# Four stacked graph layers on one core: a plan that counts changes of TensorE's tiling, and pairs a graph's scores with an older graph's weights times v

## The chip, the core and the metric

The kernel runs on one core of a Trainium2 chip. The metric is the device time of one execution in microseconds. A core has TensorE (matrix products into PSUM), VectorE (called DVE in the profile), ScalarE (ACT), GpSimd (POOL), and SyncE (SP), which here issues most DMAs. The engines run side by side, each through its own list of instructions in a fixed order, and wait for each other through semaphores.

## What is computed

There are 128 graphs of 128 nodes with 512 features, float32, and one adjacency matrix for all. Four layers follow each other; each ends in a residual sum and a normalisation over the features.

```
x = layernorm(x + L0(x))   # A = adj @ x; per node: relu(max over features of A + b)
x = layernorm(x + L1(x))   # h = x @ W; e = leaky_relu(s1 + s2) * adj; att = softmax(e)
                           # elu(att @ h + beta * h)
x = layernorm(x + L2(x))   # (adj @ x) @ weight + bias
x = layernorm(x + L3(x))   # q, k, v = x @ Wq + bq, ...; 8 heads of 64
                           # scores = q @ k.T / 8, masked where adj == 0
                           # softmax(scores) @ v
```

## The kernel before

Graphs pass through the layers one after the other in a pipeline. For a graph b, TensorE runs these steps: `l0` (one product of 128x512), `zT` (four products of 128x128 that apply the attention of layer 1 and transpose), `z` (four products of 128x512 with W), `yT` and `y` (the same pair for layer 2), then for each group of four graphs 21 steps named q, k and v, which make the three projections by seven half-size products each (`seven`), and for each graph the scores, `sc`, and the product of the softmax weights with v, `avT`. An instruction of the program is run by TensorE as two in the profile[...].

Two of these steps use half of TensorE's array at a time. In `l3_scores` (line 785) a head has 64 features, so a product uses 64 of the 128 rows, and two heads lie in the two halves of the rows. In `l3_avT` (line 871) the result of a head has 64 columns, and two heads lie in the two halves of the columns. Every other step uses the whole array. The last six graphs (`LATE`) take another way behind the scores: `l3_pT` (line 849) transposes their weights on TensorE, and `l3_av` (line 917) multiplies them in whole-array products of 65 columns.

Between `sc` and `avT` of one graph lies a long way. VectorE adds the mask to the scores (line 807, which frees the single PSUM tile of the scores and fills the single buffer `pr`) and takes each row's maximum (line 813). ScalarE takes eight exponentials (line 817). SyncE writes the weights to HBM and reads them back in another order (lines 366 and 370). VectorE finishes the transposition (line 377) into one of two buffers `pT`. After `avT`, ScalarE copies the result (line 883), it goes through HBM and VectorE in the same manner, GpSimd scales it and adds the residual (lines 896 and 897), and the last normalisation follows.

The order on every engine comes from a planner, the class `Plan`, that runs while the program is built. It keeps a clock for TensorE and simulates the other engines with a cost for each of their operations. Every step has a place in line, an expected cost, the marks (results) that it waits for, and the buffers that it takes. In `Plan.run` the clock picks, of all steps that are ready by the plan's own times, the one with the smallest place; then it adds the cost. The other engines' operations are emitted in the order in which they begin in the plan. A step's place is its graph's number plus its turn, then its position in a row:

```
row = ["av", "sc", "yT", "y", "l0", "zT", "z"]
turns = {"av": 12.5, "sc": 11.5, "yT": 3, "y": 3, "l0": 0, "zT": 2, "z": 2}
return lambda b: (b + turns[name]) * R + row.index(name)
```

So weights times v of a graph are due one round after its scores, where a round is what TensorE does for one graph. They run when the plan has them ready.

Of the kernel before, what the change touches and what calls it, by code (L numbers as in the profile page):

```python
# [22 lines left out]
class Plan:  # L23

    def __init__(self, bufs):
        self.heap, self.count = [], 0  # L30
        self.engine = {}
        self.left = dict(bufs)
        self.parked = {tag: [] for tag in bufs}
        self.marks, self.waiting = {}, {}
        self.end = 0.0
# [56 lines left out]
    def run(self, steps, total):  # L92

        nxt = {name: 0 for name in steps}
        now = 0.0
        while any(nxt[name] < total[name] for name in steps):
            self.events(now)
            best, later = None, []
            for name, (place, cost, waits, bufs, fn) in steps.items():
                b = nxt[name]  # L100
                if b >= total[name]:
                    continue
                marks = [self.marks.get(key) for key in waits(b)]
                if any(m is None for m in marks) or any(self.left[t] < n for t, n in bufs(b).items()):
                    continue
                if marks and max(marks) > now:
                    later.append(max(marks))
                elif best is None or place(b) < best[0]:
                    best = (place(b), name, b)
            if best is None:  # L110
                if self.heap:
                    later.append(self.heap[0][0])
                now = min(later)
                continue
            _, name, b = best
            place, cost, waits, bufs, fn = steps[name]
            nxt[name] += 1
            for tag, n in bufs(b).items():
                self.left[tag] -= n
            now += cost  # L120
            self.end = now + HOP
            gen = fn(b)
            self.resume(gen, self.end)
        self.events(float("inf"))
# [3 lines left out]
def kernel(  # L128
# [815 lines left out]


    row = ["av", "sc", "yT", "y", "l0", "zT", "z"]
    turns = {"av": 12.5, "sc": 11.5, "yT": 3, "y": 3, "l0": 0, "zT": 2, "z": 2}
    R = len(row)

    def place(name):  # L950
        return lambda b: (b + turns[name]) * R + row.index(name)
# [4 lines left out]
    def av_waits(b):  # L956
# [12 lines left out]
        "xT": (early("y", 1.0), 0.55, lambda b: [("x3", b)], need("mm"), l3_xT),  # L969
        **{n: (seven_place(n), 1.73, seven_waits(n), seven_bufs(n), seven(n)) for n in "qkv"},  # L970
        "sc": (
            place("sc"), 1.1,
            lambda b: [(n, b // GB, "C", r, b % GB // 2) for n in "qk" for r in range(2)],
            need("sc"), l3_scores,
        ),
# [48 lines left out]
```

## Time and profile before

| | |
|---|---|
| median of three runs | 2804.46 us (2802.49 to 2806.31) |
| profiled execution | 2803.4 us |
| its span, first to last instruction | 2801.6 us |
| mean granted clock of TensorE | 0.992 |
| TensorE busy | 2730.6 us, 97% |
| VectorE busy | 2276.3 us, 81% |
| ScalarE busy | 1573.6 us, 56% |
| GpSimd busy | 1388.1 us, 50% |
| mean busy share of the DMA engines | 47% between 100 and 2700 us |

A busy share is the time in which an engine had an instruction running, over the span. The ends of matmuls are modelled, and consecutive ones overlap[...]; the starts of matmuls are what was measured. A wait is put down to the engine and the instruction that ended it. The profile's rows name a tile by its name in the program without its number: `ps_sc` are the scores, `ps_av` weights times v, `ps_q_chain` and its like the projections, `psA` layer 0.

### The profile page before, as it was taken

What the parts mean: (1) busy time and instruction counts of PE and PEld (TensorE: products, weight loads), DVE (VectorE), ACT (ScalarE), POOL (GpSimd) and SP (SyncE); (2) the same over time, 40 slices, a digit from 0 to 9 for tenths busy, and PEclk for the clock granted to TensorE, in tenths of its full rate; (3) what the DMA queues carried; (4) which work ended last, traced back from release to release, by engine and by line L of the source; (5) the groups of instructions that cost most, each with busy time, mean ns of one, the idle gap of its engine ahead of it and who ended that gap; (6) DMA issues with size and microseconds to landing.
All of it is one profiled execution on the core that took longest, in us unless ns stands there. A gap on an engine that the chain in (4) does not pass through costs nothing.

```text
span 2801.6 us, 42968 instructions
## 1 busy us (share of the span) xinstructions
PE 2730.6 (97%) x13905; PEld 1936.2 (69%) x13905; DVE 2276.3 (81%) x4288; ACT 1573.6 (56%) x4189; POOL 1388.1 (50%) x2192
## 2 busy tenths in 40 slices
PE   6999999999999999999999999999999999999997
PEld 3677677777667666776776776776777677676776
DVE  7668888888888878888888888988888888888866
ACT  3455555555555555555555555555655555555545
POOL 4535444555445545445545455554554554455545
PEclk8999999999999999999999999999999999999998
DMA  3224444455444445445444445454454444444443
GB/s 123 59 84 140 147 130 140 142 156 152 141 149 139 144 129 158 147 138 153 149 143 152 141 144 160 144 160 145 142 162 139 134 137 148 143 147 142 138 132 125
DMA packets 459793, 392.26 MB, mean 140 GB/s; under 512 B 88752, under 2 KB 376624, under 8 KB 459568
## 3 DMA queue, kind: packets, MB, share of 16 engines
q1 hardware_dynamic: 456464, 383.74, 44.8%
q10 hardware_dynamic: 2976, 5.77, 0.6%
q8 instruction: 110, 1.80, 0.3%
q14 instruction: 115, 0.94, 0.1%
q0 software_dynamic: 128, 0.01, 0.0%
HBM read 218.17 MB, written 171.24 MB: 139 GB/s over the span
## 4 chain that ended last, share of the span: by engine, by line
PE 85%; DVE 11%; POOL 1%; DMA 1%; issue 1%; ACT 1%; SPq 0%; DVEq 0%; POOLq 0%; ACTq 0%
PE ps_z L508 14%; PE ps_y L508 13%; PE ps_q_chain L681 7%; PE ps_k_chain L681 7%; PE ps_v_chain L681 7%; PE ps_av L871 4%; PE ps_sc L785 4%; PE ps_zT L494 4%; PE ps_k_pair L681 4%; PE ps_v_pair L681 4%; PE ps_q_pair L681 3%; PE psA L390 3%; PE ps_yT L551 3%; PE ps_q_first L681 2%; DVE pT L377 2%; PE ps_v_first L681 2%
## 5 line engine op out<-in xcount | busy, mean ns | idle before, releaser
L350 POOL TENSOR_SCALAR ve<-mv 128x1 f32<-128x1 f32 x512 | 129.7, 253 | 821.8 <-DVE mv L347 723.7
L508 PE MATMUL ps_y<-w_sb,yT 128*128 128x512 f32 x1024 | 463.8, 596 | 0.5 <-ACT yT L557 0.5
L508 PE MATMUL ps_z<-w_sb,zT 128*128 128x512 f32 x1024 | 462.6, 594 | 1.6 <-ACT zT L500 1.1
L817 ACT ACTIVATE pr<-pr,nm 128x128 f32<-128x128 f32 x992 | 387.1, 393 | 77.8 <-DVE nm L813 76.8
L356 ACT ACTIVATE x<-xp,nmr,rstd 128x512 f32<-128x512 f32 x384 | 311.0, 810 | 187.8 <-POOL nmr L354 184.4
L345 DVE BATCH_NORM_STATS2 stats<-xp 128x6 f32<-128x512 f32 x512 | 345.0, 674 | 23.2 <-ACT xp L399 14.7
L508 PEld LDWEIGHTS ps_z<-w_sb,zT 128*128 128x128 f32 x1024 | 192.4, 190 | 211.0 <-issue 203.2
L508 PEld LDWEIGHTS ps_y<-w_sb,yT 128*128 128x128 f32 x1024 | 190.7, 190 | 201.6 <-issue 193.2
L352 POOL TENSOR_TENSOR rstd<-ve,nhalf 128x1 f32<-128x1 f32 x512 | 298.6, 583 | 42.7
L377 DVE STREAM_TRANSPOSE pT<-turn_pr 128x1024 f32<-128x1024 f32 x122 | 249.7, 2047 | 0.0
L412 DVE SCALAR_TENSOR_TENSOR junk<-x,wa_bc 128x512 f32<-128x512 f32 x256 | 208.5, 814 | 50.7 <-ACT x L356 49.0
L896 POOL TENSOR_TENSOR xp<-xp,rd 128x512 f32<-128x512 f32 x122 | 128.2, 1050 | 233.0 <-DVE xp L377 153.1
L521 ACT ACTIVATE elu_r<-ps_z 128x512 f32<-128x512 f32 x128 | 76.1, 594 | 269.8 <-PE ps_z L508 269.5
L537 POOL TENSOR_TENSOR x2b<-x,bias_bc 128x512 f32<-128x512 f32 x128 | 164.4, 1284 | 113.8 <-ACT x L356 109.9
L639 POOL TENSOR_TENSOR x3r<-x3r,bv_bc 128x512 f32<-128x512 f32 x128 | 170.5, 1332 | 90.3 <-DMA x3r<-turn_hbm_x 89.2
L817 ACT ACTIVATION_READ_ACCUMULATOR pr<-pr,nm 128x1 f32 x976 | 185.1, 190 | 0.0
L354 POOL TENSOR_SCALAR nmr<-mv,rstd 128x1 f32<-128x1 f32 x512 | 147.4, 288 | 53.0
L525 DVE SCALAR_TENSOR_TENSOR xp<-ps_z,x 128x512 f32<-128x512 f32 x128 | 87.8, 686 | 95.2 <-ACT elu_r L521 95.1
L897 POOL TENSOR_TENSOR xp<-xp,x3r 128x512 f32<-128x512 f32 x122 | 159.6, 1308 | 9.6
L785 PEld LDWEIGHTS ps_sc<-kTh,qTh 64*128 64x128 f32 x2048 | 124.2, 187 | 52.3 <-issue 32.2
L871 PE MATMUL ps_av<-pT,va 128*64 128x128 f32 x1952 | 135.4, 281 | 21.6 <-DVE pT L377 17.1
L871 PEld LDWEIGHTS ps_av<-pT,va 128*64 128x64 f32 x1952 | 105.9, 138 | 72.9 <-issue 30.6
(148 smaller groups left out, 5929.6 us busy)
## 6 DMA issues: line engine op xcount, KB each, us to landing
turn_hbm_pr<-pr SPq DMA_DIRECT2D x122, 512.0 KB
turn_pr<-turn_hbm_pr SPq DMA_DIRECT2D x122, 512.0 KB
x<-in_x_dram SPq DMA_DIRECT2D x128, 256.0 KB
out_dram<-xp SPq DMA_DIRECT2D x128, 256.0 KB
turn_hbm_x<-x SPq DMA_DIRECT2D x124, 256.0 KB
turn_x<-turn_hbm_x SPq DMA_DIRECT2D x124, 256.0 KB
x3r<-turn_hbm_x SPq DMA_DIRECT2D x124, 256.0 KB
turn_hbm_o<-oT SPq DMA_DIRECT2D x122, 256.0 KB
```

The lines of the kernel that those rows point to most:

```text
L345: nc.vector.bn_stats(stats, src)
L352: nc.gpsimd.tensor_tensor(rstd, ve, nhalf, ALU.pow)
L356: nc.scalar.activation(dst, src, AF.Identity, bias=nmr, scale=rstd)
L377: nc.vector.transpose(dst.rearrange("p n (c a) -> p a n c", a=NQ), t)
L412: nc.vector.scalar_tensor_tensor(junk, x1, 1.0, wa_bc[i], ALU.mult, ALU.mult, accum_out=col)
L508: nc.tensor.matmul(ps, lhsT(c), rhs(c), start=(c == 0), stop=(c == NCC - 1))
L537: nc.gpsimd.tensor_tensor(xb, x2, bias2_bc, ALU.add)
L639: nc.gpsimd.tensor_tensor(s["x3r"], s["x3r"], by_block(b, bv_bc), ALU.add)
L681: nc.tensor.matmul(ps[:, m, :], lhsT, rhs, start=fresh and m + k == 0, stop=m + k == 2, skip_group_check=not fresh)
L785: nc.tensor.matmul(ps[:, h % 2, f, :], heads["q", g][j // 2][r : r + HD, f, j % 2 * P : (j % 2 + 1) * P], heads["k", g][j // 2][r : r + HD ...
L817: nc.scalar.activation(pr_h[:, i], pr_h[:, i], AF.Exp, bias=nm[:, i : i + 1], accum_out=None if late else den[:, i : i + 1])
L871: nc.tensor.matmul(ps[e * HD : (e + 1) * HD, f * P : (f + 1) * P], va[:, 2 * f + e, 0:HD], pT[:, e * 4 + f, :], start=True, stop=True,)
```

## The change

Two of the planner's steps are declared half-array ones, `sc` of rows and `avT` of columns. The planner remembers which use of the array the last step left (`mode`), and adds 0.2 us to its clock whenever the next step has another. After a half-array step it prefers a half-array step if one is ready, one of the same kind first, and only then goes by place; after a whole-array step it goes by place as before. The turn of `av` goes from 12.5 to 14.5, so that weights times v are due three rounds after the scores, and the planned cost of `sc` from 1.1 to 0.92. No operation of any engine is edited.

```diff
+    TILED = {"sc": "rows", "avT": "columns"}
+    SWITCH = 0.2
...
-        now = 0.0
+        now, mode = 0.0, None
...
-                elif best is None or place(b) < best[0]:
-                    best = (place(b), name, b)
+                else:
+                    tiled = self.TILED.get(name)
+                    key = ((tiled is None, tiled != mode) if mode else (), place(b))
+                    if best is None or key < best[0]:
+                        best = (key, name, b)
...
-            now += cost
+            now += cost + (self.SWITCH if self.TILED.get(name) != mode else 0.0)
+            mode = self.TILED.get(name)
...
-    turns = {"av": 12.5, "sc": 11.5, "yT": 3, "y": 3, "l0": 0, "zT": 2, "z": 2}
+    turns = {"av": 14.5, "sc": 11.5, "yT": 3, "y": 3, "l0": 0, "zT": 2, "z": 2}
...
-            place("sc"), 1.1,
+            place("sc"), 0.92,
```

The diff adds nine lines ahead of the steps, so line 871 of before is line 880 after, and so on.

## The prediction

> **What bounds the kernel now.** I read the page first (engines, slices), then TensorE's waits, then its timeline around single blocks, then VectorE's timeline there.
>
> ```profile
> span 2801.6 us, 42968 instructions
> PE 2730.6 (97%) x13905; PEld 1936.2 (69%) x13905; DVE 2276.3 (81%) x4288; ACT 1573.6 (56%) x4189; POOL 1388.1 (50%) x2192
> PE   6999999999999999999999999999999999999997
> ```
>
> TensorE is busy in every slice but the first and last; the next engine, VectorE, has a fifth of its time free. So a microsecond of TensorE's own queue is a microsecond of the end, as long as what it reads arrives. "Busy" says nothing of how well it is used, so I looked at start times. In this stretch of TensorE's timeline (start, length, line, tiles):
>
> ```profile
> 1418.85 1.89 PE L681 MATMUL ps_v_chain<-sums_v,T 128*128 128x256 f32 x8
> 1420.58 1.02 PE L390 MATMUL psA<-x,adjT 128*128 128x512 f32 x2
> 1421.53 1.16 PE L785 MATMUL ps_sc<-kTh,qTh 64*128 64x128 f32 x16
> 1422.62 1.16 PE L494 MATMUL ps_zT<-attT,x 128*128 128x128 f32 x8
> 1423.71 1.09 PE L871 MATMUL ps_av<-pT,va 128*64 128x128 f32 x16
> 1424.73 1.16 PE L551 MATMUL ps_yT<-adjT,x 128*128 128x128 f32 x8
> 1425.73 1.89 PE L681 MATMUL ps_v_pair<-wv_sb,xTh 128*128 128x256 f32 x8
> 1427.46 1.02 PE L508 MATMUL ps_z<-w_sb,zT 128*128 128x512 f32 x2
> ```
>
> The lengths are modelled; the distances of starts are what the queue pays. Nothing waits here. A layer-0 product (psA) between whole-array steps takes 0.858 start to start; ahead of the scores it takes 0.95, so 0.094 more. A transposing step of eight (zT, yT) between whole-array steps takes 0.891; yT, right behind a half-array step, takes 1.00, so 0.104 more; zT, with one on both sides, takes 1.09, both surcharges. A seven-product step shows the same over the trace: 1.727 alone, 1.820 ahead of, 1.831 behind a half-array step. The scores take 1.09 and weights times v 1.02 wherever they stand. **A visit to half use therefore costs 0.198 us outside its own steps.**
>
> What a second half-array step costs when it follows directly is shown elsewhere in the same view:
>
> ```profile
> 1484.05 1.16 PE L785 MATMUL ps_sc<-kTh,qTh 64*128 64x128 f32 x16
> 1485.14 1.09 PE L871 MATMUL ps_av<-pT,va 128*64 128x128 f32 x16
> 1486.16 1.99 PE L681 MATMUL ps_k_chain<-xTh,sums_k 128*128 128x256 f32 x8
> ```
>
> Again 1.09 and 1.02, and one pair of surcharges around both: going from row tiles to column tiles adds nothing to these two lengths.
>
> TensorE's waits (engine, tile, line, releaser: total, times, longest), stretch 100 to 2700 us:
>
> ```profile
> PE ps_av L871 <- DVE pT L377: 13.5, 16, 2.4
> PE ps_av L871 <- DVE rd L466: 3.2, 4, 1.6
> PE ps_yT L551 <- ACT x L356: 0.9, 1, 0.9
> PE ps_av L871 <- DVE xp L596: 0.9, 1, 0.9
> PE ps_y L508 <- ACT yT L557: 0.5, 1, 0.5
> ```
>
> 17.6 of the 19.7 us waited there stand ahead of weights times v, whose transposed weights pT are late. Why late: the scores starting at 1421.53 above are masked only here, on VectorE:
>
> ```profile
> 1437.48 1.21 DVE L807 TENSOR_TENSOR pr<-ps_sc,mask 128x1024 f32<-128x1024 f32 x1
> ```
>
> 16 us later. Over the trace the mask starts 1.2 to 22 us after its scores (median 13), pT ends 31 to 52 us after them (median 43), and weights times v starts a median of 0.9 us after pT: the old plan asks for it the moment it is ready.
>
> [...] In the trace [...]at a change the load and its matmul start together (1421.53 and 1422.62 on both rows)[...]. [...] After the longest wait of the steady part (2.4 us, at 1021.8) the granted clock of the next 4 us is 0.58, and the two steps there take 1.5 us more than their usual length (1.91 for 1.02, 2.42 for 1.83)[...].
>
> **The change part by part.** No instruction is added or removed on any engine; only orders change.
>
> 1. Visits. I counted them in TensorE's order of both programs. Before: 128 score steps and 122 of weights times v make 230 visits (20 times the two stand together). After: 128 visits; each of the 122 weights-times-v steps stands next to a score step, 121 behind it and the last one ahead of it. 102 fewer visits × 0.198 = **20.2 us**, all on TensorE's queue. The edit of sc's cost (1.1 to 0.92) and SWITCH move only the plan's clock: a round of one graph is 18.57 us of whole-array steps plus 2.31 for a pair (1.09 + 1.02 + 0.20) = 20.9, and the plan now assumes 21.1, where it assumed 20.7 for a real 21.1. So the plan no longer errs on the safe side, by 0.2 us per round.
>
> 2. Waits for pT. After, weights times v of graph b always follows the scores of b+2 (121 of 122), two rounds or 42 us after b's own scores, against 32 to 55 before. Taken alone that would be early. But VectorE's and ScalarE's orders change too. Before, the newest TensorE result standing ahead of the mask in VectorE's order is finished a median of 8 us (up to 20) after the scores start; after, never later than the scores. Ahead of the last exponential in ScalarE's order it falls from 27 us (median) to 9. From mask to pT's end the trace has a median of 30 us and at most 36; with the mask 1.2 us behind the scores pT is there after 31, at most 38, and is wanted at 42 to 44. So the 17.6 us go, and with them the 1.5 us at half clock: **19.1 us**.
>
> 3. The later turn of av (12.5 to 14.5). It holds two pT at once (two buffers: the third is written some 30 us after the step that frees the first) and va for two more rounds (group g+2 asks for it at round 4g+18, it is freed at about 4g+16.5). No queue is passed by more work: SP and POOL issue the same DMAs and operations. I cost this at nothing; the cover is the slack just given, and without it each us is one on TensorE.
>
> 4. New waits. y comes directly behind yT with only one transposing step between in 25 graphs, before in 6. The gap is then 0.89 us, and ScalarE's copy takes 0.59. The 6 cost 0.5 us of waits; 25 in proportion cost **2.1 us**. Bounds: nothing, or one exponential of 0.58 us ahead of each copy, 14.5.
>
> 5. The end. In the last 100 us the kernel before waits 2.8 and 0.8 us for pT and 2.4 for T (with about 2 us of half clock). After, T has 22 us between y and its use where 18 were needed, but with rounds of 8 to 16 us there the weights times v of graph 119 and 120 come only 24 us after their scores, and the shortest path in the trace was 31. I take the two as equal; bounds 7 us of gain, 7 of loss.
>
> Sum from the profiled execution, which took 2803.4 (span 2801.6): 2803.4 − 20.2 − 19.1 + 2.1 = 2766.2. It lies 1.1 under the median 2804.46. I forecast **2766 us**, 1.4% less.
>
> **The rivals.** A: as summed, 2766; chance 0.72, its own range 2753 to 2776.
> B: only the visits pay. Waits for pT turn into others of like size (yT or zT copies behind the exponentials that now come at once, psum banks given back later): 2803.4 − 20.2 + 0 to 4 = 2783 to 2787. For it: five kinds of short waits already exist, and the plan's margin shrinks. Against: they come to 2.1 us. Chance 0.17.
> C: the change does not pay what I read: the two surcharges belong to half-array steps, not to visits, so a pair pays inside. Then the gain is 0 to 10 from visits with the plan's order as good as before: 2793 to 2804. The pair at 1484 and 16 more without a wait speak against. Chance 0.06.
> D, slower: VectorE does not get to mask and transposition earlier in fact. If pT kept its old delays (median 43, up to 52) and were wanted at 43, each weights-times-v step would wait 2.1 us on average (mean of what exceeds 43.1 in the trace), 122 × 2.1 = 256, about 3020. It decides the sign from 0.33 us per step (40.6 / 122). Against it: the orders in part 2, and VectorE's fifth of free time. Chance 0.05.
>
> **How the numbers follow.** The difference that a measurement of this kernel can tell is 0.2%, 5.6 us, so faster means under 2798.8. A and B are faster, most of C; D slower: faster 0.92, same 0.03, slower 0.05. The range takes A with its bounds and B: 2752 to 2788.
>
> **What would show it.** In the profile after: each score step directly followed by L880's weights times v, 2.11 us for both; yT or another step behind them 0.104 longer, none on both sides. Waits of ps_av for pT under 3 us in all until the end; the mask 1 to 3 us behind its scores. I am wrong if the mask still trails by 10 us, if ps_y or ps_z show waits above 10 us in all, or if scores behind weights times v turn out longer than 1.09.

## The result, and the profile after

The changed kernel takes **2759.8 us** (median of 5 runs, 2759.3 to 2761.2) against 2804.5 for the kernel before on the same chip: a ratio of 0.984, 95% interval 0.9826 to 0.9855. The profiled execution took 2759.3, with a span of 2757.5, 44.1 us less than before. The forecast was 2766.

The head of the page, the same three rows as before:

```profile
span 2757.5 us, 43085 instructions
PE 2707.9 (98%) x13905; PEld 1936.6 (70%) x13905; DVE 2248.3 (82%) x4288; ACT 1578.1 (57%) x4189; POOL 1391.1 (50%) x2192
PE   6999999999999999999999999999999999999997
```

TensorE bounds the kernel as before. Its timeline at the same place in a round (start, length, line, tiles):

```profile
1402.62 1.02 PE L399 MATMUL psA<-x,adjT 128*128 128x512 f32 x2
1403.57 1.16 PE L794 MATMUL ps_sc<-kTh,qTh 64*128 64x128 f32 x16
1404.67 1.09 PE L880 MATMUL ps_av<-pT,va 128*64 128x128 f32 x16
1405.69 1.16 PE L560 MATMUL ps_yT<-adjT,x 128*128 128x128 f32 x8
1406.69 1.06 PE L503 MATMUL ps_zT<-attT,x 128*128 128x128 f32 x8
1407.58 3.65 PE L517 MATMUL ps_y<-w_sb,yT 128*128 128x512 f32 x8
```

Scores and weights times v take 1.10 and 1.02 start to start, psA ahead of them 0.95 and yT behind them 1.00: one pair of surcharges for two steps. zT, which paid on both sides in the stretch before, is back at 0.89.

TensorE's waits (engine, tile, line, releaser: total, times, longest), stretch 100 to 2650 us, are two rows, and none of them is for pT:

```profile
PE ps_z L517 <- DVE xp L605: 2.6, 5, 0.6
PE ps_yT L560 <- ACT x L365: 0.9, 1, 0.9
```

And VectorE's timeline has the mask of the scores that start at 1403.57 right behind them:

```profile
1404.78 1.23 DVE L816 TENSOR_TENSOR pr<-ps_sc,mask 128x1024 f32<-128x1024 f32 x1
```

**An account of TensorE's queue.** A wait row counts only from the modelled end of the matmul before it. So for every kernel below I also took the distance of starts of each step in the stretch 100 to 2700 us, and subtracted the usual length of that step and the surcharges (0.094 ahead of a visit to half use, 0.104 behind it). What is left is time in which the queue stood still or ran at half clock.

| kernel | median us | surcharges | rest |
|---|---|---|---|
| before (turn 12.5) | 2804.5 | 43.4 | 25.2 |
| after (turn 14.5, preference) | 2759.8 | 24.4 | 9.3 |

Of the 44.1 us, 19.0 are surcharges in this stretch (20.2 with its ends) and 15.9 are the rest in it. The remaining 8 are a balance. Between the 118th score step and its last product, TensorE stood still or ran at half clock about 13 us less than before; against that, it stood still about 2 us more in the first 100 us, and what follows its last product took 2 us more.

### The profile page after: what moved, and what is told of

It reads as the page before. It is cut to its first block, busy times and chain, and to the rows that moved or that the text cites. A ratio compares the mean times of both kernels' runs of the same rounds, so it can differ in the third digit from the quotient of the medians.

```text
span 2757.5 us, 43085 instructions
## 1 busy us (share of the span) xinstructions
PE 2707.9 (98%) x13905; PEld 1936.6 (70%) x13905; DVE 2248.3 (82%) x4288; ACT 1578.1 (57%) x4189; POOL 1391.1 (50%) x2192
## 4 chain that ended last, share of the span: by engine, by line
PE 95%; DVE 2%; POOL 1%; DMA 1%; issue 0%; ACT 0%; SPq 0%; POOLq 0%; DVEq 0%
PE ps_y L517 16%; PE ps_z L517 16%; PE ps_v_chain L690 8%; PE ps_k_chain L690 8%; PE ps_q_chain L690 8%; PE ps_sc L794 5%; PE ps_yT L560 5%; PE ps_av L880 4%; PE ps_zT L503 4%; PE ps_q_pair L690 4%; PE ps_v_pair L690 4%; PE psA L399 4%; PE ps_k_pair L690 4%; PE ps_q_first L690 2%; PE ps_v_first L690 2%; PE ps_k_first L690 2%
## 5 line engine op out<-in xcount | busy, mean ns | idle before, releaser
L648 POOL TENSOR_TENSOR x3r<-x3r,bv_bc 128x512 f32<-128x512 f32 x128 | 179.1, 1400 | 245.3 <-DMA x3r<-turn_hbm_x 235.2
L421 DVE SCALAR_TENSOR_TENSOR junk<-x,wa_bc 128x512 f32<-128x512 f32 x256 | 228.4, 892 | 13.8 <-ACT x L365 12.6
L906 POOL TENSOR_TENSOR xp<-xp,x3r 128x512 f32<-128x512 f32 x122 | 169.7, 1391 | 9.6
L816 DVE TENSOR_TENSOR pr<-ps_sc,mask 128x1024 f32<-128x1024 f32 x124 | 151.0, 1218 | 23.7 <-PE ps_sc L794 22.8
L363 POOL TENSOR_SCALAR nmr<-mv,rstd 128x1 f32<-128x1 f32 x512 | 139.6, 273 | 53.0
L503 PEld LDWEIGHTS ps_zT<-attT,x 128*128 128x128 f32 x1024 | 130.6, 193 | 29.7 <-issue 26.6
```

Source lines behind the costliest of these rows:

```text
L421: nc.vector.scalar_tensor_tensor(junk, x1, 1.0, wa_bc[i], ALU.mult, ALU.mult, accum_out=col)
L503: nc.tensor.matmul(ps[:, c * P : (c + 1) * P], s["x1"][:, c * P : (c + 1) * P], attT, start=True, stop=True)
L648: nc.gpsimd.tensor_tensor(s["x3r"], s["x3r"], by_block(b, bv_bc), ALU.add)
L906: nc.gpsimd.tensor_tensor(by_block(b, xp), by_block(b, xp), s.pop("x3r"), ALU.add)
```

## The experiments

All times are medians, in each case with the kernel before run beside them (2804.4 to 2806.5); a ratio is to that kernel, with its 95% interval.

**The preference turned round, the rest kept (`unpaired`).** The planner now prefers a whole-array step behind a half-array one; `owed` remembers that the weights times v that would have followed the scores are still to come. Edit against after:

```diff
-        now, mode = 0.0, None
+        now, mode, owed = 0.0, None, False
...
-                    key = ((tiled is None, tiled != mode) if mode else (), place(b))
+                    key = (tiled is not None if mode else (tiled != "columns" if owed else 0), place(b))
...
+            owed = name == "sc" or (owed and mode is None)
```

> The plan of after (turn 14.5, SWITCH 0.2), but behind a half-array step it takes a whole-array step first, and then the weights times v that are owed: 249 visits to half use, no pairs, weights times v still 42 to 48 us behind their own scores. Theory 1 (each visit costs 0.198 us outside its steps): 121 visits more than after, +24 us, 2784 (2780 to 2788), with waits of ps_av for pT near nothing. Theory 2 (the gain is from the later turn and the tidier order alone, visits cost nothing): 2760. Theory 3 (each change of use costs some 0.095 us, rows to columns included): 249 x 2 + 1 changes against 378, +11.5 us, 2771.

Measured: 2790.6 us, ratio 0.9950 (0.9936 to 0.9965), 30.8 above after. Its TensorE timeline:

```profile
1416.24 1.02 PE L400 MATMUL psA<-x,adjT 128*128 128x512 f32 x2
1417.20 1.16 PE L795 MATMUL ps_sc<-kTh,qTh 64*128 64x128 f32 x16
1418.29 1.16 PE L504 MATMUL ps_zT<-attT,x 128*128 128x128 f32 x8
1419.38 1.09 PE L881 MATMUL ps_av<-pT,va 128*64 128x128 f32 x16
1420.40 1.16 PE L561 MATMUL ps_yT<-adjT,x 128*128 128x128 f32 x8
1421.40 1.89 PE L691 MATMUL ps_v_pair<-wv_sb,xTh 128*128 128x256 f32 x8
```

With zT between them, scores and weights times v are as long as before (1.09 and 1.02), but zT takes 1.09. The surcharges rise from 24.4 to 47.1 and the rest from 9.3 to 16.8, together 30.2. The second rise is a new wait, in the list of this kernel:

```profile
PE ps_yT L561 <- ACT x L366: 6.4, 21, 0.9
```

So the price of a visit is confirmed (121 more visits, 22.7 us in the stretch), theory 2 is out, and theory 3 gives half of what the starts show. The result lies 2.6 us above the range of theory 1; what exceeds its 2784 is not the visits' but, for the most part, the new wait's.

**The preference alone (`pref_only`).** Edit against after:

```diff
-    turns = {"av": 14.5, "sc": 11.5, ...
+    turns = {"av": 12.5, "sc": 11.5, ...
```

> After with the turn of av back at 12.5, so only the counting and the preference for half-array steps: 130 visits, but weights times v come as soon as the plan has them ready, with a median of 9 us of TensorE's time between the last TensorE result ahead of pT in VectorE's order and the step (before 7, after 20). Theory 1: the visits' 20 us are gained and most of the 21 us of waits for pT stay: 2776 to 2788. Theory 2: no gain from fewer visits, 2795 to 2804. A third possibility, that pairing alone also removes the waits: 2760 to 2766.

Measured: 2815.6 us, ratio 1.0038 (1.0025 to 1.0051). None of the three: it is **slower than before**, with 130 visits. Surcharges fall to 24.1, the rest rises to 63.1. Its waits:

```profile
PE ps_av L880 <- DVE pT L386: 33.8, 25, 3.7
PE ps_yT L560 <- ACT x L365: 9.2, 10, 1.2
PE ps_z L517 <- DVE xp L605: 5.5, 6, 1.0
```

The row for pT in the same list of before is half of that, and the waits in all eat more than the 20 us:

```profile
PE ps_av L871 <- DVE pT L377: 17.1, 18, 2.8
```

Half clock comes on top: the mean granted clock of the profiled execution is 0.989 here and 0.992 in before. The last section comes back to it.

**The later turn alone (`turn_only`).** Edit against before:

```diff
-    turns = {"av": 12.5, "sc": 11.5, ...
+    turns = {"av": 14.5, "sc": 11.5, ...
```

> Before with the turn of av at 14.5 and nothing else: 247 visits, weights times v 57 to 60 us behind their scores, mask no later than the scores in VectorE's order. Theory 1: waits for pT gone (-21 us) and those at the end (-8), 17 visits more (+3.4), some new short waits (0 to 6): 2778 to 2785. Theory 2 (the order does all): about 2760. If the later turn only moves the waits elsewhere: 2800 to 2808.

Measured: 2784.2 us, ratio 0.9927 (0.9913 to 0.9942), inside theory 1. Surcharges 47.2, rest 8.5. Its list has no row of L871 waiting for pT; between 100 and 2650 us TensorE waits for these alone:

```profile
PE ps_yT L551 <- ACT x L356: 0.9, 1, 0.9
PE ps_v_pair L681 <- DVE va L716: 0.8, 2, 0.4
PE ps_v_chain L681 <- ACT st_v L701: 0.2, 1, 0.2
```

The pairing is worth 24.4 us on top of it (2784.2 to 2759.8), and costs 11.2 without it (2804.4 to 2815.6).

**One round less (`turn135`), and that alone (`turn135_only`).** Turn 13.5 with the preference, against after, and without it, against before:

```diff
-    turns = {"av": 14.5, "sc": 11.5, ...
+    turns = {"av": 13.5, "sc": 11.5, ...
```

> After with the turn of av at 13.5: 128 visits as in after, weights times v 40 to 42 us behind their scores, 17 us behind the last TensorE result ahead of pT in VectorE's order. Theory 1: one round of the two would have been enough, 2757 to 2763, and fewer short waits if the order is more regular. Rival: the second round is needed, waits of ps_av for pT of 5 us or more return, 2766 to 2780.

> Before with the turn of av at 13.5 and no preference: 229 visits, weights times v 41 to 50 us behind their scores, but the mask still trails its scores in VectorE's order (median 11 us) and pT has 8 us of TensorE's time ahead of its use. Theory A (what removes the waits is the regular order, in which mask and exponentials come at once, and not the lateness of weights times v by itself): the waits stay, 2797 to 2806. Theory B (a round more of lateness is enough): waits for pT go, 2778 to 2786.

Measured: 2751.5 us, ratio 0.9809 (0.9792 to 0.9825), with the preference: better than after by 8.3, since the rest falls to 2.4. That is theory 1, with more gain than its 2757 to 2763. Without the preference 2806.6, ratio 1.0004 (0.9995 to 1.0013): no difference, and the waits for pT stay:

```profile
PE ps_av L871 <- DVE pT L377: 17.2, 25, 1.7
```

That is theory A, half a microsecond above its range: one round of lateness by itself removes no wait while the mask trails, and it does trail (median 15 us, against 1.2 in `turn135`). So the second round was not needed once the steps are paired, and one round alone does nothing. In `turn135_only` weights times v still start a median of 1.0 us after pT ends; in `turn_only` 28 us after, in `turn135` 12, in after 15.

**The plan's cost of one transposition (`pref12_pt`, `before_pt`).** The plan takes 1.25 us for VectorE's transposition of pT; the trace of before has 2.05 (122 of them, 1.97 to 2.13). Edit against `pref_only`, and the same against before:

```diff
-        yield dve({1: 0.3, 4: 0.7, 8: 1.25}[n])
+        yield dve({1: 0.3, 4: 0.7, 8: 2.05}[n])
```

> The kernel with the preference and the turn at 12.5 (2815.6), with one planned cost corrected: the transposition of pT at 2.05 us, as the trace has it, instead of 1.25. 128 visits. Theory A (with av due at once, weights times v are placed where the plan first has pT ready, and any error of the plan is a wait on TensorE; this cost is a main one): waits of ps_av for pT fall from 34 us to 10 or less, 2780 to 2792. Theory B (the cause is the tight place itself, other delays of the same size take over): 25 us or more of waits for pT, 2805 to 2820.

> Before with the planned cost of the transposition of pT at 2.05 us instead of 1.25 and nothing else: turn 12.5, no preference, 234 visits, the mask still a median of 8.5 us behind its scores in VectorE's order. Theory A (a step placed where the plan first has its input ready pays for the plan's errors, and this cost is the main one): waits of ps_av for pT fall from 17 us to under 5, less 15 to 21 us, 4 visits more (+0.8): 2784 to 2791. Theory B (the late mask and the irregular order make the waits, whatever the cost of this one step): 15 us or more of waits, 2800 to 2808.

Measured: `pref12_pt` 2750.3 us, ratio 0.9802 (0.9788 to 0.9817), 65.3 below `pref_only` by one number in the plan; `before_pt` 2784.9, ratio 0.9925 (0.9909 to 0.9942). Waits for pT of the first and of the second:

```profile
PE ps_av L880 <- DVE pT L386: 1.8, 1, 1.8
```

```profile
PE ps_av L871 <- DVE pT L377: 4.5, 3, 3.5
```

Theory A in both, for `pref12_pt` with 30 us more gain than its range of 2780 to 2792. In `before_pt` the mask still starts a median of 13.6 us behind its scores and pT ends 43.4 us behind them, as in before (12.9 and 43.3). Only the median time from pT's end to its use grew, from 0.9 to 1.8 us, by about what was added to the cost.

**A dose, and the plan's other error (`pref12_pt165`, `pref12_sw01`).** Both against `pref_only`:

```diff
-        yield dve({1: 0.3, 4: 0.7, 8: 1.25}[n])     # pref12_pt165
+        yield dve({1: 0.3, 4: 0.7, 8: 1.65}[n])
...
-    SWITCH = 0.2                                    # pref12_sw01
+    SWITCH = 0.1
```

> The preference with the turn at 12.5, SWITCH 0.2, and the planned cost of the transposition of pT at 1.65 us, half way between 1.25 (2815.6) and 2.05 (2750.3); 128 visits. If each wait is the error of the plan for that one step, half of it is left: waits for pT of 10 to 20 us, 2770 to 2790. If another property of the order decides: near one of the two ends, under 2758 or over 2805.

> The preference with the turn at 12.5 (2815.6), SWITCH 0.1 instead of 0.2: again 130 visits, but a round of the plan is 20.8 us, no longer 0.2 above the chip's 20.9. Theory A (the plan's clock of TensorE runs slower than the chip's, so that what is ready in the plan is late on the chip, and this made the waits worse than before's 17 us): waits for pT fall from 34 us to 10 to 20, 2780 to 2795. Theory B (the cost of the transposition alone makes them): 25 us or more, 2803 to 2820.

Measured: 2764.8 us, ratio 0.9853 (0.9837 to 0.9870), for half the correction; 2772.6, ratio 0.9882 (0.9867 to 0.9896), for the smaller SWITCH at an uncorrected transposition. The waits for pT, in this order:

```profile
PE ps_av L880 <- DVE pT L386: 9.7, 14, 1.2
```

```profile
PE ps_av L880 <- DVE pT L386: 10.1, 21, 2.4
```

The first lies a little below its forecast of 2770 to 2790, nearer to the full correction than half. The second speaks for its theory A, with 7 us more gain than its range: with 130 visits in both, a plan whose round is 20.8 instead of 21.1 us loses 43 us less. The plan adds SWITCH three times for a pair, into the scores, from rows to columns and out, 0.6 us in all, where the chip pays 0.20.

**The same two edits where there is slack (`turn135_sw01`, `turn135_pt`).** Against `turn135`: SWITCH 0.1, and the transposition at 2.05.

> The kernel with the preference and the turn at 13.5 (2751.5), with SWITCH 0.1 instead of 0.2, so that a round of the plan is 20.8 us where the chip's is 20.83. Theory A (the plan's error of 0.3 us per round is harmless where each result has some us to spare): 2749 to 2754. Theory B (the plan then errs on the safe side and short waits go): 2746 to 2749, no more than the 2.4 us of waits left between 100 and 2700.

> The kernel with the preference and the turn at 13.5 (2751.5), with the planned cost of the transposition of pT at 2.05 us. 128 visits, weights times v 38 to 43 us behind their scores. Theory A (slack covers the error): 2749 to 2754, no difference. Theory B (a truer plan orders better everywhere, the end included): 2742 to 2748.

Measured: 2752.1 us, ratio 0.9807 (0.9793 to 0.9822), and 2755.8, ratio 0.9821 (0.9805 to 0.9837). Neither gains: where pT is ready 12 us before its use, the plan's errors don't reach TensorE. The second lies 4 us above `turn135`, just outside its theory A. It has 3 us more of rest in the stretch; why this order has them was not tried.

## Why the prediction was right, and where it was not

The sum of the prediction's steps, with what the traces show for each:

| step | predicted | measured |
|---|---|---|
| 1. visits | −20.2 | −20.2 (−19.0 from 100 to 2700 us) |
| 2. waits for pT and half clock | −19.1 | −21.3 |
| 4. new short waits | +2.1 | +5.4 |
| 5. the end (what remains of the account) | 0 | −8 |
| sum | −37.2 | −44.1 |

The forecast came within some 6 us because of step 1 and the body of step 2. That the rest came so close is partly luck: step 4 came out 3.3 us worse and steps 2 and 5 together 10.2 us better, and these pull against each other.

*Step 1* held: 102 visits fewer, and the starts in after show the same two surcharges (0.094 and 0.104 us) on every kind of neighbour that a pair has there. They belong to the visit, and going from rows to columns costs nothing outside the two steps: in after, 121 pairs have the same 1.09 and 1.02. So the surcharge of a change shows between whole and half use alone. The `unpaired` kernel gave the surcharges back. Rival C is out, and so is rival B: the new short waits came to 5.4 us, where it needed some 20.

*Step 2*: the waits are gone as said, and on the path that was forecast. The size was 2.2 short, because the rows of the wait list begin at a modelled end; from start to start the waits ahead of weights times v in before were 19.8 us, with 1.5 of half clock behind one of them. The path, as medians over the graphs in us (the first three columns count from the start of a graph's scores, the last is the listed total over the whole trace):

| kernel | mask starts | pT ends | weights times v start | from pT's end to their start | waits for pT |
|---|---|---|---|---|---|
| before | 12.9 | 43.3 | 44.1 | 0.9 | 17.1 |
| `turn135_only` | 15.0 | 44.7 | 46.3 | 1.0 | 17.2 |
| `pref_only` | 9.8 | 40.3 | 40.9 | 0.5 | 33.8 |
| `before_pt` | 13.6 | 43.4 | 45.8 | 1.8 | 4.5 |
| `pref12_pt` | 7.6 | 38.1 | 39.9 | 1.8 | 1.8 |
| after | 1.2 | 27.9 | 42.1 | 15.2 | none |
| `turn135` | 1.2 | 28.3 | 39.9 | 11.9 | none |
| `turn_only` | 2.2 | 30.5 | 59.1 | 28.2 | none |

In after, weights times v start no later behind their scores than before. The 15 us between pT and its use come from the earlier pT (28 us, where the step had 31), and 11.7 of the 15.4 us that pT gains are the prompt mask's. `turn135_only`, with a later turn and a mask that trails, gains nothing.

What the step had **wrong** is the trailing mask as the reason for the waits of before. `before_pt` keeps the trailing mask and pT's 43 us, and loses its waits all the same, but for 4.5 us. What made the waits is that weights times v stood in the queue where the plan first had pT ready, while the plan took the transposition 0.8 us too short. The true cost gives back that 0.8 us. A prompt mask gives far more, and no kernel in the table that has one lists a wait for pT; but the mask was never moved by itself, and why the plan brings it forward with the later turn stays open. (The prediction has some slips that its sum doesn't rest on. The 27 and 9 us given as medians for the last exponential are upper quartiles; the medians are 23.6 and 6.5. The short waits other than those of weights times v are of four kinds, not five. And the gain that rival D has to eat up is the sum's own 37.2 us, or 0.30 us per step, not 40.6.)

The signs that the prediction named came out: no row for pT, a mask 1.2 us behind the scores, and 3.7 us in all of waits of y and z.

*The change to the plan's clock in step 1* was seen (0.2 us a round on the unsafe side) and priced at nothing. With 15 us between pT and its use that was right, as far as is known: in `turn135`, with 12 us, SWITCH made no difference (in after it was not varied). At turn 12.5 it was worth 43 us. The mechanism of rival D, a step that asks for pT before it is there, is what `pref_only` shows, with its sign; the later turn in the same change is what kept the whole clear of it.

*Step 3*, the later turn at no cost, was right as far as buffers go. Yet it was one round too much: `turn135` is 8 us faster, 6.9 of it short waits in the stretch.

*Step 4* had the wrong place. y behind yT does not wait once in after's list. The 5.4 us are what the rest of after (9.3) has above that of before without step 2's share (25.2 − 21.3). The largest part is z, which waits until VectorE has read a PSUM tile (2.6 in the list above, 3.5 from start to start); smaller ones stand ahead of yT and the scores.

*Step 5* was mis-sized. The pT of graph 119 is late as feared, but it stalls TensorE by 0.05 us only: it came 23.9 us behind its scores, where the shortest in the old trace was 31, since nothing stood ahead of the mask. The waits in the last 100 us of before (2.8, 2.4, 1.6, 1.0 and 0.8, with a granted clock of 0.50 for 6.8 us behind the 2.8 and for 10.2 us behind the 1.6) became 0.3, 0.2 and 0.9. The 8 us are the remainder of the account, with small losses at the start and behind the last product in them; the end was not tried by itself.

**The best versions found.** `pref12_pt` (2750.3) and `turn135` (2751.5) beat both kernels, by 1.9 to 2.0% against before, and are not told apart by these runs. What is left in `turn135` between 100 and 2700 us is 24.4 of surcharges and 2.4 of rest.

## What to carry to other kernels

Read the price of a change from distances of starts, on both sides of it: here the whole surcharge of using half the array (0.094 and 0.104 us) stood in the rows of the two neighbours, and two half-array steps side by side share it. A planner that places a step the moment its input is ready turns each error in its costs into a wait on the engine that bounds the kernel, so compare its costs with the trace, and look there how long an input lies ready before its use. Here a median of 0.5 to 1 us went with 17 to 34 us of waits, and 11 us or more with none. An edit that saves 20 us of queue can lose 30 if it moves a step to where its input is not yet there; judge it together with the due time.

## What the runs showed of the hardware

A visit to half use of TensorE costs 0.094 us ahead of the half-array step and 0.104 behind it. In before that holds for six kinds of neighbour, start to start:

| neighbour | between whole-array steps | ahead of a half-array step | behind one |
|---|---|---|---|
| psA | 0.858 | 0.952 | 0.963 |
| zT, yT | 0.89 | 0.984 | 0.995 |
| a seven-product step | 1.727 | 1.820 | 1.831 |
| z, y | 3.433 | 3.527 | 3.538 |

In after psA (0.952), yT (0.984 and 0.995), y (3.537) and a seven-product step (1.820 and 1.831) have the same. What makes the two surcharges was not shown. The half-array steps' own lengths, 1.09 and 1.02, are the same in both traces whether the neighbour is whole or half. A whole-array step that starts behind a wait is longer too: 0.104 us in three of before (ahead of each stood a whole-array step), 0.075 to 0.104 in the six of after. A half-array step is not (a median of 0.000 in the 21 cases of before).

The length of a wait alone does not decide whether half clock follows. A wait of 2.4 us brought it in before, and one of 3.4 us did not in `pref_only`, as the lengths of these steps show (1.98 and 1.09 us):

```profile
1024.25 1.98 PE L871 MATMUL ps_av<-pT,va 128*64 128x128 f32 x16 [2.44 <-DVE pT L377]
```

```profile
1370.39 1.09 PE L880 MATMUL ps_av<-pT,va 128*64 128x128 f32 x16 [3.41 <-DVE pT L386]
```

In before the granted clock was 0.50 from 1024.0 to 1027.4 us, behind that wait, and 1.00 on both sides of it. The other half-clock stretches of before and after that ended within the span lasted 6.8, 10.2, 6.8 and 10.2 us (before) and 20.5 us (after). What tells the two waits apart was not shown. In the last 100 us it came with less: in after a wait of 0.87 us ended at 2739.9, and the granted clock was 0.50 from 2741.0 to the end.
